# Moving a group norm off VectorE in a convolution kernel by codes

## The chip, the cores and the metric

The kernel runs on one core of a Trainium2 chip. The metric is device time in microseconds (us), the median of three runs; lower is better. Five engines work side by side, each with its own queue: TensorE (PE) for matrix products, VectorE (DVE), ScalarE (ACT), GpSimd (POOL) and SyncE (SP, which here only issues transfers). ScalarE and GpSimd issue transfers as well.

## The reference, cut to what matters

Sixteen images of 256 channels and 28x28 pixels. Each is normalised by groups of 8 channels, then passes two 3x3 convolutions by codes (every channel's 3x3 patch is softly assigned to 16 centroids), then a gate from channel means, and is added to the input.

```python
def amm_conv3x3(x, centroids, w_sub):
    p = patches(x, 3, 3)                                   # b, pixel, channel, 9
    d = sum(p*p) - 2*einsum('bncs,cks->bnck', p, centroids) + sum(centroids*centroids)
    attn = softmax(-d)                                     # over 16 centroids
    lut = einsum('cks,cso->cko', centroids, w_sub)
    return einsum('bnck,cko->bno', attn, lut)

def _gn(v, G=32, eps=1e-5):
    g = v.reshape(B, G, C // G, H, W)
    m, s = mean(g, (2, 3, 4)), var(g, (2, 3, 4))
    return (g - m) / sqrt(s + eps)

h   = _gn(x)
out = relu(bn1(amm_conv3x3(h, centroids1, wsub1)))
out = bn2(amm_conv3x3(out, centroids2, wsub2))
out = se_layer(out)                                        # channel gate
result = x + relu(out + h)
```

## The kernel before

The work is laid out in slots. A stage is one layer of one image: 2 pieces of 392 or so pixels times 11 groups of channels, 22 slots. Stages follow as layer 0 of image b+1, layer 1 of image b, and so on, 32 stages in all. In a slot TensorE computes the codes (`logits`), the numerators of the group before (`b_num`), and three or four "looks" (`c_look`, the product with the weights); ScalarE takes exponentials; VectorE transposes; GpSimd scales. Layer 1 needs the maximum of the codes first for three of its groups (`MAXED`): those are computed six slots ahead (`a_logits`, `a_turn`, `a_max`), which loads TensorE and above all VectorE in some slots.

```python
ring = [p_ring.tile([P, 2, 512], F32, name=f"pair{i}") for i in range(3)]   # PSUM, three pairs of banks
turn = [0]
def pair():
    turn[0] += 1
    return ring[turn[0] % 3]
def bank():
    return pair()[:, 0]
...
def logits(u, gi, rows):                        # two pairs of the ring
    ps = [pair(), pair()]
    ...
def a_turn(u, gi):                              # two transposes on VectorE
    for ps in u.pop(("lg", gi)):
        z = tpool.tile([P, 832], F32, tag="z", name="z")
        nc.vector.transpose(..., ps[:, :, : 32 * nb])
def b_exp(u, gi):
    for ps in u.pop(("lg", gi)):
        nc.scalar.activation(e[:, :, :n], ps[:, :, :n], AF.Exp, scale=2.0)
def b_num(u, gi):                               # one pair of the ring
    ps = pair()
    ...
def b_turn(u, gi):                              # on VectorE: transpose, reciprocal, two reductions
    ...
```

Group norm in four steps, one slot each, on VectorE with two small products on TensorE:

```python
def gn_stats(b):
    st = small.tile([P, NB, 2, 6], F32, name="gn_st")
    mv = small.tile([P, NB, 2], F32, name="gn_mv")
    for k in range(NB):                         # two blocks of 128 channels
        for i in range(2):
            nc.vector.bn_stats(st[:, k, i, :], xs[b][:, k, i * (HW // 2) : (i + 1) * (HW // 2)])
        nc.vector.bn_aggr(mv[:, k, :], st[:, k])
def gn_mean(b):
    ps = bank()[:, : 2 * NB]
    nc.tensor.matmul(ps, lhsT=gmat, rhs=mv, ...)
    nc.vector.tensor_copy(gm, ps)
    nc.vector.tensor_sub(dv, mv[:, :, 0], gm[:, :, 0])
    nc.vector.tensor_mul(dv, dv, dv)
def gn_var(b):
    ps = bank()[:, :NB]
    nc.tensor.matmul(ps, lhsT=gmat, rhs=dv, start=True, stop=True)
    nc.vector.tensor_add(var, gm[:, :, 1], ps)
    rsqrt(rstd, var, GN_EPS, NB)                # two operations on GpSimd
def gn_apply(b):
    for k in range(NB):
        nc.vector.tensor_scalar(ims[0][:, k, ...], xt[:, k], gm[:, k, 0:1], rstd[:, k : k + 1], op0=ALU.subtract, op1=ALU.mult)
```

The normed image is copied with a shift of one column to each side (`shift`, ScalarE) and written to memory as patterns (`to_pat`, transfers issued by ScalarE), from which `patches` (issued by GpSimd) loads the operands of the codes.

```python
class Plan:
    def prep(self, l, pat, t, near):
        for i, dx in enumerate((0, 2)):
            for k in range(NB):
                self.at(t + i, 4 + 2 * k, shift, l, dx, k)
        for i in range(len(STEPS)):             # 12 steps
            self.at(t + 1 + (i // 2 if near else i), 8, to_pat, l, i, pat)
    def norm(self, b, t):
        for k, f in enumerate((gn_stats, gn_mean, gn_var, gn_apply)):
            self.at(t + k, 9, f, b)
...
clear_pat(0)                                    # at the start: transfers issued by ScalarE
...
for f in (gn_stats, gn_mean, gn_var, gn_apply): # the first image, in the setup
    f(0)
...
        if l == 0 and b >= 1:
            t0 = t - NS + (1 if b == 1 else -6)
            plan.at(t0 - 1, 9, load_x, b, x[b])
            plan.norm(b, t0 + 1)
            plan.prep(0, pat_of(0, b), t0 + 5, False)
...
    plan.at(18, 9, setup_codes, 1)              # needs GpSimd and TensorE
```

`at(slot, pos, ...)` puts a step into a slot; steps of a slot go out in the order of `pos`, and each engine keeps that order.

Of the kernel before, what the change touches and what calls it, by code (L numbers as in the profile page):

```python
# [8 lines left out]
F32 = mybir.dt.float32  # L9
AF = mybir.ActivationFunctionType  # L10
ALU = mybir.AluOpType
# [4 lines left out]
P = 128  # L16
H = W = 28
HW = H * W
# [61 lines left out]
def kernel(  # L80
# [32 lines left out]
    nc = tc.nc  # L113
    B, C, _ = x.shape
    NB = C // P
# [5 lines left out]
    small = ctx.enter_context(tc.tile_pool(name="small", bufs=3))  # L121
# [8 lines left out]
    ring = [p_ring.tile([P, 2, 512], F32, name=f"pair{i}") for i in range(3)]  # L130
# [5 lines that stand above are left out]

    def bank():
        return pair()[:, 0]

    def view(t, off, dims):  # L140

        return bass.AP(t.tensor, t.offset + off, [list(d) for d in dims])

    d_pat = [dram.tile([NRT * 32, HW], F32, name=f"pat{i}") for i in range(3)]
# [4 lines left out]
    xs = {}  # L149

    def load_x(b, xb):
        t = xpool.tile([P, NB, HW], F32, tag="xt", name="xt")
        nc.gpsimd.dma_start(t, xb.rearrange("(b p) n -> p b n", p=P))
        xs[b] = t
# [52 lines left out]
    ims = [const.tile([P, NB, NPAD], F32, name=f"im{l}") for l in range(2)]  # L207
# [28 lines left out]
    def rsqrt(dst, src, eps, n):  # L236

        t = small.tile([P, n], F32, name="rs_t")
        nc.gpsimd.tensor_scalar(t, src, eps, None, op0=ALU.add)
        nc.gpsimd.tensor_tensor(dst, t, mhalf[:, :n], ALU.pow)  # L240
# [19 lines left out]
    def sort_channels():  # L260
# [12 lines left out]
        nc.vector.tensor_mul(key, key, t)  # L273

        ps = bank()
        for b in range(NB):
            dg = scratch(P)
# [136 lines left out]
    gst = {}  # L414
    nrm = {}

    def gn_stats(b):
        st = small.tile([P, NB, 2, 6], F32, name="gn_st")
        mv = small.tile([P, NB, 2], F32, name="gn_mv")
        for k in range(NB):  # L420
            for i in range(2):
                nc.vector.bn_stats(st[:, k, i, :], xs[b][:, k, i * (HW // 2) : (i + 1) * (HW // 2)])  # L422
            nc.vector.bn_aggr(mv[:, k, :], st[:, k])
        gst[b] = mv

    def gn_mean(b):
        mv = gst[b]
        ps = bank()[:, : 2 * NB]
        nc.tensor.matmul(ps, lhsT=gmat, rhs=mv.rearrange("p b t -> p (b t)"), start=True, stop=True)
        gm = small.tile([P, NB, 2], F32, name="gn_gm", bufs=6)  # L430
        nc.vector.tensor_copy(gm.rearrange("p b t -> p (b t)"), ps)
        dv = small.tile([P, NB], F32, name="gn_dv")
        nc.vector.tensor_sub(dv, mv[:, :, 0], gm[:, :, 0])
        nc.vector.tensor_mul(dv, dv, dv)
        gst[b] = gm, dv

    def gn_var(b):
        gm, dv = gst.pop(b)
        ps = bank()[:, :NB]
        nc.tensor.matmul(ps, lhsT=gmat, rhs=dv, start=True, stop=True)  # L440
        var = small.tile([P, NB], F32, name="gn_var")
        nc.vector.tensor_add(var, gm[:, :, 1], ps)
        rstd = small.tile([P, NB], F32, name="gn_rstd", bufs=6)
        rsqrt(rstd, var, GN_EPS, NB)
        nrm[b] = gm, rstd

    def gn_apply(b):
        gm, rstd = nrm[b]
        xt = xs.pop(b)
        for k in range(NB):  # L450
            nc.vector.tensor_scalar(
                ims[0][:, k, W : W + HW], xt[:, k], gm[:, k, 0:1], rstd[:, k : k + 1], op0=ALU.subtract, op1=ALU.mult
            )

    def shift(l, dx, k):

# [24 lines left out]
    se = {}  # L481

    def se_hidden(b):
        _, ysum = ys[b]
        ps = bank()[:, :1]
        n = 0
        for k in range(NB):
            for i in range(2):
                nc.tensor.matmul(
                    ps[0:RED], lhsT=w1_sb[:, k, :], rhs=ysum[:, k, i : i + 1],  # L490
                    start=(n == 0), stop=(n == 2 * NB - 1),
                )
                n += 1
        hid = small.tile([RED, 1], F32, name="se_hid")
        nc.scalar.activation(hid, ps[0:RED], AF.Relu, bias=b1_sb, scale=1.0 / HW)
        se[b] = hid

    def se_gate(b):
        hid = se.pop(b)
        ps = bank()[:, :NB]  # L500
        for k in range(NB):
            nc.tensor.matmul(
                ps[:, k : k + 1], lhsT=w2_sb[:, k * P : (k + 1) * P], rhs=hid, start=True, stop=True
            )
        gt = small.tile([P, NB], F32, name="se_gt")
        for k in range(NB):
            nc.scalar.activation(
                gt[:, k : k + 1], ps[:, k : k + 1], AF.Exp, bias=nb2_sb[:, k : k + 1], scale=-1.0
            )
        se[b] = gt  # L510

    def se_scale(b):
        gt = se[b]
        nc.vector.tensor_scalar_add(gt, gt, 1.0)
        nc.vector.reciprocal(gt, gt)
        gm, rstd = nrm[b]
        nb = small.tile([P, NB], F32, name="se_nb")
        nc.vector.tensor_mul(nb, gm[:, :, 0], rstd)
        nc.vector.tensor_scalar_mul(nb, nb, -1.0)
        se[b] = gt, nb  # L520

    def half(k, i):
        return slice(None), k, slice(i * (HW // 2), (i + 1) * (HW // 2))

    def gate(b, k, i):

        gt, nb = se[b]
        y = ys[b][0][half(k, i)]
        nc.scalar.activation(y, y, AF.Identity, bias=nb[:, k : k + 1], scale=gt[:, k : k + 1])  # L529

    def finish(b, k, i):

        y, xt = ys[b][0][half(k, i)], xs[b][half(k, i)]
        _, rstd = nrm[b]
        nc.vector.scalar_tensor_tensor(y, xt, rstd[:, k : k + 1], y, op0=ALU.mult, op1=ALU.add)  # L535
        nc.vector.scalar_tensor_tensor(y, y, 0.0, xt, op0=ALU.max, op1=ALU.add)  # L536

# [210 lines left out]
    NS = len(PXT) * NG  # L748
# [3 lines left out]
    class Plan:  # L752
# [59 lines left out]
        def prep(self, l, pat, t, near):  # L812
            for i, dx in enumerate((0, 2)):
                for k in range(NB):
                    self.at(t + i, 4 + 2 * k, shift, l, dx, k)
            for i in range(len(STEPS)):
                self.at(t + 1 + (i // 2 if near else i), 8, to_pat, l, i, pat)

        def norm(self, b, t):
            for k, f in enumerate((gn_stats, gn_mean, gn_var, gn_apply)):  # L820
                self.at(t + k, 9, f, b)

        def close(self, b, ob, te):
            self.at(te + 1, 9, se_hidden, b)
# [14 lines left out]
    def pat_of(l, b):  # L839
        if l == 0:  # L840
            return d_pat[2 if b == 1 else 0]
        return d_pat[0 if b == B - 1 else 1]

    for f in (gn_stats, gn_mean, gn_var, gn_apply):
        f(0)
    for i, (dx, pieces) in enumerate(STEPS):
        if dx != 1 and pieces == (0,):
            for k in range(NB):
# [21 lines left out]
    plan = Plan(4, 6)  # L870
    for t in exts:
        nc.vector.memset(t, 1.0)
    for si, (l, b) in enumerate(stages):
        t = si * NS
        plan.stage(l, b, pat_of(l, b), t, *((PAIRS, ()) if l == 0 else (MIXED, MAXED)), exts[si % 2])
        if l == 0 and b >= 1:
            t0 = t - NS + (1 if b == 1 else -6)
            plan.at(t0 - 1, 9, load_x, b, x[b])
            plan.norm(b, t0 + 1)
            plan.prep(0, pat_of(0, b), t0 + 5, False)  # L880
        if l == 1:
            near = b in (0, B - 1)
            plan.prep(1, pat_of(1, b), t - NS + (LC + 1 if near else 0), near)
            plan.at(t + NS + LC, 9, load_x, b, x[b])
            plan.close(b, out[b], t + NS + LC)
# [9 lines left out]
    ps = bank()  # L895
# [6 lines left out]
    with tc.If(flag > 0):  # L902
        with tc.For_i(0, B) as bi:
            load_x("g", x[bass.ds(bi, 1)].rearrange("o c n -> (o c) n"))
            plan = Plan(1, 4)
            plan.norm("g", 0)
            plan.prep(0, d_pat[0], 4, False)
            plan.stage(0, "g", d_pat[0], 30, PAIRS, ORDER, None)
            plan.prep(1, d_pat[1], 30 + NS + LC, False)
            s1 = 30 + NS + LC + 26  # L910
            plan.stage(1, "g", d_pat[1], s1, PAIRS, ORDER, None)
            plan.at(s1 + NS + LC, 9, load_x, "g", x[bass.ds(bi, 1)].rearrange("o c n -> (o c) n"))
            plan.close("g", out[bass.ds(bi, 1)].rearrange("o c n -> (o c) n"), s1 + NS + LC)
            plan.emit()
# [76 lines left out]
```

## Time and profile before

| | us |
|---|---|
| median of three runs | 3277.77 (3275.5 to 3278.19) |
| span of the profiled execution | 3267.5 |
| TensorE busy | 3106.2 |
| VectorE busy | 2527.0 |
| ScalarE busy | 1475.2 |
| GpSimd busy | 1313.0 |
| first codes of the first stage | at 106.80 |

The profile is one execution, read in several views. The engine table gives busy times; the slices show them along the span in tenths; the groups by line give count and mean duration of one kind of instruction; the timeline lists instructions in order (start, duration, engine, line, operation, output <- inputs, shape, count, and in brackets how long the engine had been idle and what ended that); the windows give busy time and granted TensorE clock in a stretch. Matrix products run pipelined, so a busy TensorE need not be at its full speed, and its lost time is best seen as the distance between the starts of its blocks.

### The profile page before, as it was taken

The numbers are of one execution on the slowest core, as the hardware profiler recorded it, in microseconds if no ns is written. First come the engines' busy times: TensorE is split into PE (matmuls) and PEld (weight loads), VectorE is DVE, ScalarE is ACT, GpSimd is POOL, SyncE is SP. The second block draws the span as 40 slices with busy tenths as digits, with TensorE's granted clock in tenths as the row PEclk, the third lists the DMA queues.
The fourth block names the chain that finished last, engine by engine and source line by source line (L and its number), as shares of the span: only waits on it lengthen the run. The fifth ranks groups of instructions, "written<-read, shape, count | busy, mean of one in ns | idle before, by whom it ended". The sixth has DMA issues, their size and how long they took to land.

```text
span 3267.5 us, 72362 instructions
## 1 busy us (share of the span) xinstructions
PE 3106.2 (95%) x29086; PEld 1214.2 (37%) x29086; DVE 2527.0 (77%) x4261; ACT 1475.2 (45%) x2443; POOL 1313.0 (40%) x1347
## 2 busy tenths in 40 slices
PE   4489999999999999999999999999999999999997
PEld 3133333333333333333333333333333333333333
DVE  2266878788787878878787887879788787878786
ACT  1144454444545444454444445444444545445343
POOL 1133444443434434343444434444443444434342
PEclk8699999999999999999999999999999999999999
DMA  7566555565655556565555656655565665556532
GB/s 239 122 183 198 179 183 183 156 204 172 219 184 172 188 156 195 181 213 178 172 182 155 218 177 202 192 164 187 155 226 177 195 194 163 181 166 218 175 104 69
DMA packets 232374, 586.03 MB, mean 179 GB/s; under 512 B 76238, under 2 KB 89182, under 8 KB 232030
## 3 DMA queue, kind: packets, MB, share of 16 engines
q0 software_dynamic: 76544, 321.16, 31.5%
q10 hardware_dynamic: 82666, 238.70, 22.2%
q1 hardware_dynamic: 72820, 21.45, 3.1%
q8 instruction: 232, 3.80, 0.5%
q14 instruction: 112, 0.92, 0.1%
HBM read 328.23 MB, written 257.82 MB: 179 GB/s over the span
## 4 chain that ended last, share of the span: by engine, by line
PE 73%; DVE 17%; DMA 5%; POOL 3%; issue 2%; ACT 1%; ACTq 0%; SPq 0%; POOLq 0%; DVEq 0%
PE acc L719 39%; PE pair L568 18%; PE pair L642 14%; DVE nt L654 4%; DVE q L708 3%; DVE rc L658 3%; POOL nt L681 3%; DVE y L535 2%; DMA xt<-in_x 1%; DMA pat<-side 1%; DVE gn_st L422 1%; DVE z L587 1%; DVE y L536 1%; DMA dm<-mt 1%; PE pair L336 1%
## 5 line engine op out<-in xcount | busy, mean ns | idle before, releaser
L719 PE MATMUL acc<-q,ws 128*128 128x384 f32 (+1 forms) x4608 | 1742.1, 513 | 0.5 <-ACT y L742 0.5
L632 ACT ACTIVATE e<-pair 128x768 f32<-128x768 f32 (+1 forms) x1408 | 1087.4, 822 | 1450.0 <-PE pair L568 1373.6
L681 POOL TENSOR_TENSOR nt<-nt,rc 128x648 f32<-128x648 f32 (+1 forms) x576 | 772.9, 1342 | 1466.4 <-DVE rc L658 1130.4
L719 PEld LDWEIGHTS acc<-q,ws 128*128 128x128 f32 x4608 | 814.2, 190 | 915.8 <-issue 470.2
L708 DVE STREAM_TRANSPOSE q<-nt 128x768 f32<-128x768 f32 (+1 forms) x576 | 578.5, 1004 | 413.9 <-POOL nt L681 367.6
L654 DVE STREAM_TRANSPOSE nt<-pair 128x768 f32<-128x768 f32 (+1 forms) x704 | 692.4, 983 | 143.4 <-PE pair L642 140.2
L642 PE MATMUL pair<-e,cw 64*32 64x384 f32 (+1 forms) x11264 | 641.8, 507 | 52.1 <-ACT e L632 43.4
L568 PE MATMUL pair<-pt,wd 31*64 31x384 f32 (+1 forms) x9216 | 564.3, 519 | 23.9 <-DVE z L587 23.9
L658 DVE RECIPROCAL rc<-nt 128x72 f32<-128x72 f32 (+1 forms) x704 | 438.5, 623 | 24.3
L687 POOL TENSOR_TENSOR qx<-nt,rc 128x324 f32<-128x324 f32 (+3 forms) x256 | 178.9, 737 | 392.0 <-DVE rc L658 392.0
L568 PEld LDWEIGHTS pair<-pt,wd 31*64 31x64 f32 x9216 | 144.7, 131 | 420.5 <-issue 343.3
L642 PEld LDWEIGHTS pair<-e,cw 64*32 64x32 f32 x11264 | 131.1, 105 | 422.3 <-ACT e L632 200.7
L697 ACT COPY nt<-qx 128x120 f32<-128x120 f32 (+1 forms) x576 | 184.4, 320 | 187.8 <-DVE rc L658 186.3
L553 POOL DMA_DIRECT2D pt<-pat x288 | 227.4, 790 | 43.6 <-DMA pat<-side 43.2
L568 PE MATMUL pair<-pm,wd 31*64 31x384 f32 (+1 forms) x3584 | 237.9, 513 | 4.4 <-DVE z L587 3.7
L587 DVE STREAM_TRANSPOSE z<-pair 128x768 f32<-128x768 f32 (+1 forms) x192 | 182.4, 987 | 67.3 <-PE pair L568 67.3
L593 DVE TENSOR_REDUCE mx<-z 128x48 f32<-128x768 f32 (+1 forms) x192 | 186.1, 969 | 0.0
L661 DVE TENSOR_REDUCE ext<-rc 128x1 f32<-128x72 f32 (+1 forms) x608 | 140.6, 231 | 20.8
L662 DVE TENSOR_REDUCE ext<-rc 128x1 f32<-128x72 f32 (+1 forms) x608 | 134.1, 221 | 0.0
L568 PEld LDWEIGHTS pair<-pm,wd 31*64 31x64 f32 x3584 | 60.7, 129 | 165.1 <-issue 66.6
L553 POOL DMA_DIRECT2D pm<-pat x128 | 95.3, 745 | 6.3 <-DMA pat<-side 6.3
L535 DVE SCALAR_TENSOR_TENSOR y<-xt,gn_rstd,y 128x392 f32<-128x392 f32 x64 | 76.9, 1202 | 0.8 <-ACT y L529 0.8
(105 smaller groups left out, 724.0 us busy)
## 6 DMA issues: line engine op xcount, KB each, us to landing
pt<-pat POOLq DMA_DIRECT2D x144, 800.0 KB, 7.4
pt<-pat POOLq DMA_DIRECT2D x144, 768.0 KB, 5.3
pat<-side ACTq DMA_DIRECT2D x128, 771.8 KB
pat<-im ACTq DMA_DIRECT2D x64, 771.8 KB
pat<-side ACTq DMA_DIRECT2D x64, 404.2 KB
pm<-pat POOLq DMA_DIRECT2D x64, 400.0 KB, 5.7
xt<-in_x POOLq DMA_DIRECT2D x32, 784.0 KB, 8.1
pm<-pat POOLq DMA_DIRECT2D x64, 384.0 KB, 4.3
```

The lines of the kernel that those rows point to most:

```text
L553: nc.gpsimd.dma_start(pt[:, : 2 * len(gs), :n], view(u["pat"], 2 * gs[0] * P * HW + px, [[HW, P], [P * HW, 2 * len(gs)], [1, n]]),)
L568: nc.tensor.matmul(ps[i // 2][64 * h : 64 * h + 64, i % 2, :n], lhsT=wd[l][32 * i : 32 * i + rows, 2 * g + h, :], rhs=u["pt"][32 * i : 32 ...
L587: nc.vector.transpose(z[:, : 64 * nb].rearrange("p (i m) -> p i m", i=2), ps[:, :, : 32 * nb])
L593: nc.vector.tensor_reduce(u["mx"][:, a : a + 2].rearrange("p i (c b) -> p i b c", c=2)[:, :, :nb], u["z", gi].pop(0)[:, : 64 * nb].rearran ...
L632: nc.scalar.activation(e[:, :, :n], ps[:, :, :n], AF.Exp, scale=2.0)
L642: nc.tensor.matmul(ps[32 * i : 32 * i + 32, h, :n], lhsT=cw[l][64 * h : 64 * h + 64, g, i, :], rhs=es[i // 2][64 * h : 64 * h + 64, i % 2, ...
L654: nc.vector.transpose(t[:, : 2 * nb].rearrange("p (h b) r -> p h (b r)", h=2), u.pop(("nm", gi))[:, :, : 32 * nb])
L658: nc.vector.reciprocal(rc[:, : 2 * nb], t[:, : 2 * nb, SUM : SUM + 3])
L681: nc.gpsimd.tensor_tensor(v, v, rc[:, : 2 * nb].unsqueeze(3).to_broadcast([P, 2 * nb, 3, 9]), ALU.mult)
L697: nc.scalar.copy(u["nt", gi][0][:, : 2 * nb].rearrange("p (h b) r -> p h b r", h=2)[:, :, :, SUM:], bass.AP(w.tensor, w.offset, [list(w.ap ...
L708: nc.vector.transpose(q[:, : 64 * nb], t[:, : 2 * nb].rearrange("p b r -> p (b r)"))
L719: nc.tensor.matmul(accs[key][:, :n], lhsT=ws[l][:, 2 * g + h, o * P : (o + 1) * P], rhs=u["q", gi][:, 32 * nb * h : 32 * nb * h + n], star ...
```

## The change

Group norm is taken apart and moved. The statistics are taken block by block in two slots instead of in one, with the second in a slot that has no maxima before or in it. The pass over the image becomes an activation on ScalarE (`rstd * x + nb`), for which `nb = -mean * rstd` is computed once and shared with the gate. The small steps go from VectorE to ScalarE (copies out of PSUM) and GpSimd (arithmetic). The small products of group norm and gate no longer take a new pair of the ring: they use the second bank of the pair taken last (`spare`), which the exponentials have just read, so the ring keeps its turn. The shifts move to the end of a slot, behind its exponentials, and the patterns of image 1 are written in six slots instead of twelve.

```diff
+    def spare():
+        return ring[turn[0] % 3][:, 1]
...
-    def gn_stats(b):
-        ...
-        for k in range(NB):
-            for i in range(2):
-                nc.vector.bn_stats(st[:, k, i, :], ...)
-            nc.vector.bn_aggr(mv[:, k, :], st[:, k])
+    def gn_stats(b, k):
+        ...
+        for i in range(2):
+            nc.vector.bn_stats(st[:, i, :], xs[b][:, k, i * (HW // 2) : (i + 1) * (HW // 2)])
+        nc.vector.bn_aggr(gst[b][:, k, :], st)
     def gn_mean(b):
-        ps = bank()[:, : 2 * NB]
+        ps = spare()[:, : 2 * NB]
         nc.tensor.matmul(ps, lhsT=gmat, ...)
-        nc.vector.tensor_copy(gm, ps)
+        nc.scalar.copy(gm, ps)
-        nc.vector.tensor_sub(dv, mv[:, :, 0], gm[:, :, 0])
-        nc.vector.tensor_mul(dv, dv, dv)
+        nc.gpsimd.tensor_sub(dv, mv[:, :, 0], gm[:, :, 0])
+        nc.gpsimd.tensor_mul(dv, dv, dv)
     def gn_var(b):
-        ps = bank()[:, :NB]
+        ps = spare()[:, :NB]
-        nc.vector.tensor_add(var, gm[:, :, 1], ps)
+        nc.scalar.copy(var, ps)
+        nc.gpsimd.tensor_add(var, var, gm[:, :, 1])
         rsqrt(rstd, var, GN_EPS, NB)
+        nc.gpsimd.tensor_mul(nb, gm[:, :, 0], rstd)
+        nc.gpsimd.tensor_scalar(nb, nb, -1.0, None, op0=ALU.mult)
-    def gn_apply(b):
-        for k in range(NB):
-            nc.vector.tensor_scalar(ims[0][...], xt[:, k], gm[:, k, 0:1], rstd[:, k : k + 1], op0=ALU.subtract, op1=ALU.mult)
+    def gn_apply(b, k):
+        nc.scalar.activation(ims[0][...], xs[b][:, k], AF.Identity, bias=nb[:, k : k + 1], scale=rstd[:, k : k + 1])
...
     def se_hidden(b):          # and se_gate
-        ps = bank()[...]
+        ps = spare()[...]
     def se_scale(b):
         ...
-        nc.vector.tensor_mul(nb, gm[:, :, 0], rstd)
-        nc.vector.tensor_scalar_mul(nb, nb, -1.0)
...
     def prep(self, l, pat, t, near):
-                    self.at(t + i, 4 + 2 * k, shift, l, dx, k)
+                    self.at(t + 1 + i, 8, shift, l, dx, k)
     def norm(self, b, t):
-        for k, f in enumerate((gn_stats, gn_mean, gn_var, gn_apply)):
-            self.at(t + k, 9, f, b)
+        self.at(t, 9, gn_stats, b, 0)
+        self.at(t + 2, 9, gn_stats, b, 1)
+        self.at(t + 3, 9, gn_mean, b)
+        self.at(t + 4, 9, gn_var, b)
+        self.at(t + 5, 8, gn_apply, b, 0)
+        self.at(t + 6, 8, gn_apply, b, 1)
...
-            t0 = t - NS + (1 if b == 1 else -6)
-            plan.at(t0 - 1, 9, load_x, b, x[b])
-            plan.norm(b, t0 + 1)
-            plan.prep(0, pat_of(0, b), t0 + 5, False)
+            t0 = t - NS + (1 if b == 1 else -5)
+            plan.at(t0 - 2, 9, load_x, b, x[b])
+            plan.norm(b, t0)
+            plan.prep(0, pat_of(0, b), t0 + 6, b == 1)
```

## The prediction

> **What bounds the kernel now.** I read the page's engine table and slices first, then the groups by line and shape, the timeline around a group norm beside one stretch without it, the windows for the granted clock, and last the timeline of the setup.
>
> ```profile
> PE 3106.2 (95%) x29086; PEld 1214.2 (37%) x29086; DVE 2527.0 (77%) x4261; ACT 1475.2 (45%) x2443; POOL 1313.0 (40%) x1347
> ...
> PE   4489999999999999999999999999999999999997
> ```
>
> TensorE (PE) is busy 95% of 3267.5 us. The idle part is mostly in the first three slices, the setup. After it a slice is at 9, so a change on other engines can only win back what PE still loses. In a calm stretch a block of 16 products has one fixed length, so the losses can be counted: this is PE in the first layer of the last image, beside which no further image is left to normalise, from the numerators of slot 18 to those five slots on.
>
> ```profile
> 3011.74 0.91 PE L642 MATMUL pair<-e,cw 64*32 64x400 f32 x16
> 3012.58 1.21 PE L568 MATMUL pair<-pt,wd 31*64 31x400 f32 x16
> 3013.71 1.61 PE L719 MATMUL acc<-q,ws 128*128 128x400 f32 x4
> ...
> 3032.82 0.88 PE L642 MATMUL pair<-e,cw 64*32 64x384 f32 x16
> ```
>
> These five slots take 3032.82 - 3011.74 = 21.08 us. The same five slots, taken likewise from the timeline in the 14 stages that hold a group norm (images 2 to 15), take 23.85 to 28.58, mean 25.92. So group norm costs 4.84 us an image and 14 x 4.84 = 67.7 us in all: that is the ceiling of the change in the steady part. Here is where it goes, in an image without a dropped clock:
>
> ```profile
> 2053.06 1.03 DVE L422 BATCH_NORM_STATS2 gn_st<-xt 128x6 f32<-128x392 f32 x2
> ...
> 2053.93 0.91 PE L642 MATMUL pair<-e,cw 64*32 64x400 f32 x16
> ...
> 2055.39 1.79 DVE L587 STREAM_TRANSPOSE z<-pair 128x768 f32<-128x768 f32 x2
> ...
> 2056.37 1.76 PE L568 MATMUL pair<-pt,wd 31*64 31x400 f32 x16 [1.53 <-DVE z L587]
> ```
>
> The statistics stand at the end of slot 17 (slots counted in the stage), just ahead of slot 18, whose maxima pass needs two transposes (z) on VectorE (DVE). Those start 2.33 us late (2053.06 to 2055.39), and the codes' products (L568) wait for them, as their two ring pairs are the ones being transposed. Numerators to codes is 2.44 us here against 0.84 in the calm stretch, codes to looks 1.70 against 1.13: 1.60 + 0.57 = 2.17 lost to 2.33 us of VectorE work. Nearly one for one, so VectorE has no slack in these slots.
>
> ```profile
> 511.00:521.00 10.00, 8.46 (x73) 0.83 0.27 85
> ...
> 895.00:906.00 11.00, 8.92 (x72) 0.71 0.27 79
> ...
> 2052.00:2062.00 10.00, 8.47 (x90) 1.00 0.27 85
> ...
> 3008.00:3018.00 10.00, 9.90 (x95) 1.00 0.26 85
> ```
>
> These are windows of PE over the statistics: length, PE busy, granted clock. The first two lost clock as well as time; 9 of the 14 do (0.71 to 0.85), four stay at 1.00, the first has 0.98.
>
> [...]
>
> **The change part by part.** *VectorE, per image.* Removed: two passes (L451) of 1.182 = 2.36, the copy of the means 0.16, the two operations for dv 0.23 + 0.16, the variance add 0.15, and the two nb operations at the gate 0.21 + 0.17; 3.4 us in sum, 55 us over 16 images. Kept: statistics, 4 x 0.545 + 2 x 0.209 = 2.6 us of records, 2.33 end to end.
>
> *The statistics in two slots.* Block 0 stays at the end of slot 17, block 1 goes to the end of slot 19. The z of slot 18 starts 1.17 us sooner, and of the 2.17 lost there 1.0 remains. The other 1.17 us sits in front of slot 20, which has no maxima but follows a slot whose second maximum (0.95) and mt transpose (0.31) come late; slot 21 has its own two transposes. Adding VectorE's durations in order from slot 18's transposes (q 1.0, nt 1.0, reciprocal 0.64, ext 0.45, maximum 0.95 each) puts the nt of slot 20 about 0.8 us after PE wants that pair. I book 0.7 us for slot 21 over the calm stretch. Before, slots 19 to 21 lost more in such an image: 25.08 - 21.08 = 4.0, less 2.17, leaves 1.8.
>
> *The pass and the small ones.* On ScalarE 784 elements cost 0.712 + 392 x 0.875 ns = 1.06 us, an estimate; the slope is that of L742, (695 - 681) / 16 ns an element. They fall in slots 22 and 23, one each. ScalarE has about 1.1 us free between a slot's fill and the next exponentials (887.14 to 888.16 in one, filled there by other work), and exponentials end some 0.5 us before the looks. So it nearly fits; I book 0.3 us for it and for the two shifts that now stand together in one slot (2 x 0.82). The two small products stay on PE, 0.42 together. GpSimd gets five operations of about 0.22, 1.1 us an image, at 40% busy: nothing. The bank of the last exponentials no longer turns the ring, so codes don't wait for a small VectorE copy; that is inside the 1.8 above.
>
> *Late input.* In four images the statistics start late as x is still arriving. The load keeps its slot (15), so this stays: 0.3 us a mean image, with the clock drops that remain.
>
> Sum over the calm stretch: 1.0 + 0.7 + 0.3 + 0.4 + 0.3 = 2.7 instead of 4.84. Gain 2.1 x 14 = 30 us.
>
> *The first stage.* Image 1 gets its patterns in half as many slots (8 to 13 instead of 7 to 18). Before, GpSimd waited for the last of them ahead of the code setup, and PE for GpSimd:
>
> ```profile
> 213.31 1.38 POOL L681 TENSOR_TENSOR nt<-nt,rc 128x702 f32<-128x702 f32 x1 [2.18 <-DVE rc L658]
> 219.77 0.79 POOL L553 DMA_DIRECT2D pt<-pat  x1 [5.08 <-DMA pat<-side]
> 220.58 2.23 POOL L399 TENSOR_TENSOR sq<-wd 128x352 f32<-128x352 f32 x3
> ```
>
> That gives back 5.1 us and about 1 us of half clock. But where the kernel already writes patterns at the doubled rate (283 to 299 us), exponentials waited 4.63 and 5.49 us behind ScalarE's own issues, and PE's blocks lost some 5 us. Net -1 us.
>
> *The setup.* The first group norm's copies now stand in ScalarE's queue behind the clearing of the patterns:
>
> ```profile
> 3.79 20.24 ACTq L167 DMA_DIRECT2D pat<-in_consts  x6
> 24.14 11.33 ACTq L474 DMA_DIRECT2D pat<-im  x5
> ```
>
> VectorE copied the means at 16.98 and had the normed image at 21.72, before ScalarE's queue was free at 24.03. Now the chain starts at 24.05: copy 0.2, dv 0.45, product 0.6, copy 0.3, add 0.2, rsqrt 1.0, nb 0.45, two passes 2.1 = 5.3, so the first pattern leaves at about 29.5, not 24.14. ScalarE's queue then holds the weight copies (PE waited 11.3 us for L328), so most of 5.4 reaches the end; loads that use the free transfer engines meanwhile give some back. I book +4 us.
>
> Total: 3277.8 - 30 - 1 + 4 = 3251.
>
> **Rivals.** *ScalarE becomes the bound.* Passes (2.1 us), copies (0.4) and paired shifts delay exponentials, and PE waits for those instead. For: exponentials have only 0.5 us of slack in a slot of six look products. Against: ScalarE is 45% busy, and in the contested slots VectorE is late anyway, so the waits overlap. Fully paid, 14 x 2.5 = 35 us eat the gain: about 3285. *The loss disappears.* If 1.17 us of VectorE at a time is absorbed, and with shorter stalls no clock is lost, 14 images cost only the 0.42 of products: 14 x 4.4 = 62 gained, time 3219. [...] Against: one-for-one loss in slot 18. *The statistics only move their wait.* If slot 21 pays the full 1.17 and more, each image gains what the pass cost, about 1.3: 18 us, time 3263.
>
> **Range and chances.** Centre 3251. The steady gain is 15 to 50 us by the rivals, setup and first stage together 0 to +9. That gives 3228 to 3270. Over 2% faster needs below 3213.5, past even the second rival: 0.04. Over 2% slower needs above 3343, for which I see no mechanism: 0.02. Within 2%: 0.94.
>
> **What would show it.** The five slots should take about 23.8 us instead of 25.92, with 1.0 us still lost at slot 18's codes on z, and fewer than five images with a dropped clock. VectorE busy should fall by some 55 us, ScalarE rise by about 40. In the setup the first pattern issue (24.14) should come near 29.5, and the first codes (106.80) about 4 us later. PE's 7.91 us wait for sq should fall to about 3. I am wrong if the five slots stay over 25 us with exponentials as what PE waits for, if they fall under 22, or if the setup does not move.

## The result and the profile after

| | before | after |
|---|---|---|
| median, us | 3277.31 | 3248.85 (3242.53 to 3254.78) |
| ratio, 95% interval | | 0.9914 (0.989 to 0.9937) |
| span of the profiled execution | 3267.5 | 3240.9 |
| first codes | 106.80 | 116.43 |
| stage 0, its numerators to those of stage 1 | 134.37 | 141.06 |
| stages 2 to 29, likewise | 2686.2 | 2644.7 |
| stages 1 and 30, and stage 31 to the end of the span | 337.9 | 336.5 |

The changed kernel is 28.5 us faster, 0.9%; 3251 was predicted. The rows below the span split the profile: 9.6 and 6.7 us are lost ahead of stage 1, 41.5 us are won in stages 2 to 29. (The 2.2 us from the first codes to the first numerators are in no row, and are the same in both.) The last row's 1.4 us were not followed up. Here is the page, engine table and TensorE's slices:

```profile
PE 3079.0 (95%) x29086; PEld 1208.6 (37%) x29086; DVE 2479.0 (76%) x4133; ACT 1506.0 (46%) x2507; POOL 1330.1 (41%) x1427
...
PE   3489999999999999999999999999999999999997
```

VectorE lost 48.0 us of busy time and ScalarE gained 30.8. TensorE has the same 29086 products in 27 us less, and its first slice has gone from 4 to 3: the setup is what became longer.

The timeline around the statistics, in an image whose input was in time:

```profile
2230.71 1.03 DVE L426 BATCH_NORM_STATS2 gn_st<-xt 128x6 f32<-128x392 f32 x2
...
2231.58 0.90 PE L645 MATMUL pair<-e,cw 64*32 64x400 f32 x16
...
2231.90 1.79 DVE L590 STREAM_TRANSPOSE z<-pair 128x768 f32<-128x768 f32 x2
...
2232.88 1.77 PE L571 MATMUL pair<-pt,wd 31*64 31x400 f32 x16 [0.40 <-DVE z L590]
...
2234.58 1.61 PE L722 MATMUL acc<-q,ws 128*128 128x400 f32 x4
```

VectorE is 1.19 us behind slot 18 (2230.71 to 2231.90) and no longer 2.33. Numerators to codes is 1.30 us, 0.46 over the calm stretch; codes to looks 1.70, 0.57 over. Together 1.03 are lost. In the view of the waits, TensorE's waits for z fell from 27.6 us (20 waits) to the first of these lines (us in total, times, longest):

```profile
PE pair L571 <- DVE z L590: 10.5, 14, 1.8
...
PE pair L571 <- DVE nt L657: 5.4, 14, 0.5
```

The kernel before has the second of these waits once (0.5 us). Here it belongs to the second block, in slot 20 of 13 of the 14 images (all but the one that loses its clock):

```profile
2242.03 0.99 DVE L426 BATCH_NORM_STATS2 gn_st<-xt 128x6 f32<-128x392 f32 x2
...
2244.11 1.01 DVE L657 STREAM_TRANSPOSE nt<-pair 128x832 f32<-128x832 f32 x1
...
2244.51 0.28 PE L432 MATMUL pair<-gn_mv,gmat 128*128 128x4 f32 x2
2245.17 0.91 PE L571 MATMUL pair<-pm,wd 31*64 31x384 f32 x16 [0.38 <-DVE nt L657]
```

The block stands ahead of the transpose nt, and TensorE's next codes wait for nt. From its numerators to those of slot 21, slot 20 takes 6.17 us, 5.60 in the calm stretch. The five slots take 23.30 us on average over the 14 images, before 25.92; the calm stretch is unchanged (21.09). The windows over the statistics (length, PE busy, granted clock, DMA share, GB/s):

```profile
527.00:537.00 10.00, 9.60 (x93) 1.00 0.35 95
...
904.00:914.00 10.00, 9.08 (x92) 1.00 0.28 88
...
2039.00:2050.00 11.00, 9.60 (x88) 0.84 0.30 83
```

The third is the only one of 14 with a dropped clock; before there were nine. Now ScalarE's timeline in the setup ("ACTq" is its transfer queue):

```profile
3.80 19.11 ACTq L171 DMA_DIRECT2D pat<-in_consts  x6
22.95 0.16 ACT L434 COPY gn_gm<-pair 128x4 f32<-128x4 f32 x1 [20.64 <-DMA pat<-in_consts]
...
26.55 1.97 ACT L456 ACTIVATE im<-xt,gn_nb,gn_rstd 128x784 f32<-128x784 f32 x2 [2.04 <-POOL gn_nb L451]
27.62 6.63 ACTq L481 DMA_DIRECT2D pat<-im  x5
```

The copy of the means came at 22.95, behind the clearing of the patterns (before, VectorE's came at 16.98), and the first pattern left at 27.62, not 24.14. And in the first stage:

```profile
198.96 8.05 ACTq L481 DMA_DIRECT2D pat<-side  x3
207.11 1.57 ACT L635 ACTIVATE e<-pair 128x800 f32<-128x800 f32 x2 [10.32 <-DMA pat<-side]
```

Three pattern issues held ScalarE, which computed nothing for 10.32 us ahead of these exponentials, and TensorE lost 10.5 us in slots 12 to 15. Against that stands the wait that the doubled rate was to remove:

```profile
237.65 2.95 POOL L403 TENSOR_TENSOR sq<-wd 128x352 f32<-128x352 f32 x4
238.49 4.33 PE L405 MATMUL pair<-sq,nhalf_sb 128*128 128x352 f32 x8 [2.53 <-POOL sq L403]
```

It fell from 7.91 to 2.53 us, half of what the late exponentials cost.

### The profile page after: what moved, and what is told of

It is laid out like the page before. It is cut to its first block, busy times and chain, and to the rows that moved or that the text cites. A ratio compares the mean times of both kernels' runs of the same rounds, so it can differ in the third digit from the quotient of the medians.

```text
span 3240.9 us, 72313 instructions
## 1 busy us (share of the span) xinstructions
PE 3079.0 (95%) x29086; PEld 1208.6 (37%) x29086; DVE 2479.0 (76%) x4133; ACT 1506.0 (46%) x2507; POOL 1330.1 (41%) x1427
## 4 chain that ended last, share of the span: by engine, by line
PE 70%; DVE 17%; DMA 6%; POOL 3%; issue 2%; ACT 1%; SPq 0%; ACTq 0%; POOLq 0%; DVEq 0%
PE acc L722 38%; PE pair L571 17%; PE pair L645 13%; DVE nt L657 4%; DVE q L711 4%; POOL nt L684 3%; DVE rc L661 3%; DVE y L538 2%; DMA xt<-in_x 1%; DVE z L590 1%; DMA pat<-in_consts 1%; DVE gn_st L426 1%; DVE y L539 1%; DMA ws<-dws 1%; DMA dm<-mt 1%
## 5 line engine op out<-in xcount | busy, mean ns | idle before, releaser
L571 PE MATMUL pair<-pm,wd 31*64 31x384 f32 (+1 forms) x3584 | 224.9, 513 | 6.9 <-DVE nt L657 5.4
```

Source lines behind the costliest of these rows:

```text
L571: nc.tensor.matmul(ps[i // 2][64 * h : 64 * h + 64, i % 2, :n], lhsT=wd[l][32 * i : 32 * i + rows, 2 * g + h, :], rhs=u["pt"][32 * i : 32 ...
```

## The experiments

Times are medians, beside the kernel before on the same chip, with the 95% interval of the ratio. The stage lengths of each profile are used to place a difference, as a median moves by several us between runs (those of the changed kernel lie from 3242.53 to 3254.78). They have a spread too: the changed kernel, E1, E2 and E12 share one steady part and took 2643.9 to 2651.3 us in stages 2 to 29, so a smaller difference there is read from single slots, each from its numerators to those of the next. All edits are to the changed kernel. There is no E8.

### E1: the first image's group norm on VectorE again

```diff
-    gn_mean(0); gn_var(0)                     # and gn_apply(0, k): ScalarE and GpSimd
+    nc.vector.tensor_copy(gm0, ps0)           # the operations of the kernel before,
+    nc.vector.tensor_sub(dv0, ...)            # products in spare()
+    ...
+    nc.vector.tensor_scalar(ims[0][...], xs[0][:, k], gm0[...], rstd0[...], op0=ALU.subtract, op1=ALU.mult)
```

> The changed kernel with one part undone: the group norm of the first image, in the setup, is done by VectorE as before; all later images as changed. My theory: the setup of the changed kernel is 9.6 us longer (first codes at 115.9 instead of 106.3 us) as the copies stand behind ScalarE's transfers, GpSimd's chain holds up the code setup, and the loads of the weight parts, which share its buffers, then meet the pattern writes. First codes should come back to 106 to 107 us, and the time fall by 8 to 10 us, to about 3239 (0.9885 of before). Rival: the delay comes from the two passes on ScalarE and the order of the shifts alone, and the weight parts are late for another reason; then under 5 us come back.

3245.53 us (0.9914, 0.9889 to 0.9938). The first codes came at 110.13 us, 6.3 us earlier than in the changed kernel, but not at the 106 to 107 expected; stages 2 to 29 took 2643.9. Its setup:

```profile
24.14 11.79 ACTq L481 DMA_DIRECT2D pat<-im  x5
...
57.44 0.93 ACT L332 COPY ws<-pair 128x256 f32<-128x256 f32 x3 [12.99 <-DMA pat<-side]
```

The first pattern leaves at 24.14 as before, and the weight copies come at 57.44 instead of 61.91. The median alone, 3 us lower, would show nothing. But four kernels of this study have the first image on VectorE (first codes 107.05 to 112.62, mean 110.0) and eight have it on ScalarE and GpSimd (115.17 to 118.66, mean 116.9), and the two sets don't overlap: the place of this group norm costs 6.9 us. The other 3 us to the 106.80 of the one profile of before are less than the spread of the first set (5.6).

### E2: image 1's patterns in twelve slots

```diff
-            t0 = t - NS + (1 if b == 1 else -5)
+            t0 = t - NS + (0 if b == 1 else -5)
...
-            plan.prep(0, pat_of(0, b), t0 + 6, b == 1)
+            plan.prep(0, pat_of(0, b), t0 + 6, False)
```

> The changed kernel with the patterns of image 1 written in twelve slots (7 to 18) again instead of six; group norm of that image one slot earlier to make room. My theory: writing at double rate fills ScalarE's transfer queue, and exponentials wait behind it (10.3 us at one place), which costs stage 0 some 11 us, while the wait of GpSimd that it was to remove cost 5 to 6. Expected: stage 0 about 134 to 136 us instead of 141, time 5 to 7 us lower, about 3243. Rival: the wait of GpSimd for the last pattern (5.1 us, and TensorE's 7.9 behind it) comes back in full and nothing is gained: 3249, within 2 us.

3242.0 us (0.9895, 0.9873 to 0.9918); stage 0 took 135.79 us instead of 141.06, as the theory of the blocked ScalarE had it (5.3 us less). Over all runs the eight kernels with six slots have 137.84 to 145.33 (mean 141.0), the four with twelve (three of them with other moves as well) 132.14 to 135.79 (mean 134.3), and before had 134.37. So the doubled rate costs the first stage 6.7 us net of the wait that it shortens.

### E3: the pass on VectorE again, in the same slots

```diff
-        nc.scalar.activation(ims[0][...], xs[b][:, k], AF.Identity, bias=nb[...], scale=rstd[...])
+        nc.vector.tensor_scalar(ims[0][...], xs[b][:, k], rstd[...], nb[...], op0=ALU.mult, op1=ALU.add)   # b >= 1
```

> The changed kernel with the pass over the image on VectorE again for images 1 to 15 (same slots, 22 and 23, one block each; one operation with rstd and nb). My theory: VectorE has no slack between slots 18 and 36, where layer 1's maxima stand every third slot, so 2.4 us of VectorE work per image cost 1 to 2 us of TensorE: 14 to 28 us more, 3263 to 3277. Rival: the gain came from splitting the statistics and from the bank, and the pass is free in these slots: under 4 us more.

3263.32 us (0.9964, 0.9949 to 0.998); stages 2 to 29 took 2663.6, 18.9 more. The timeline shows where:

```profile
2089.19 0.96 DVE L461 TENSOR_SCALAR im<-xt,gn_rstd,gn_nb 128x784 f32<-128x784 f32 x1
...
2090.96 1.84 DVE L595 STREAM_TRANSPOSE z<-pair 128x768 f32<-128x768 f32 x2
...
2091.99 1.74 PE L576 MATMUL pair<-pm,wd 31*64 31x384 f32 x16 [0.65 <-DVE z L595]
```

This is slot 24, the first of the next stage with maxima. VectorE reaches its transposes late, behind the pass and a small step that E9 brings up, and the codes wait. The slot takes 4.72 us and not 3.60: 1.12 x 14 = 15.7 of the 18.9. The rest is in the five slots (23.52), in images whose input was late.

### E4: both blocks of statistics in one slot

```diff
-        self.at(t + 2, 9, gn_stats, b, 1)
+        self.at(t, 9, gn_stats, b, 1)
```

> The changed kernel with both blocks' statistics at the end of slot 17 again, all else as changed. My theory: the second block's 1.17 us stands in front of slot 18's two transposes and costs 1.0 to 1.2 us there, and the longer stall brings back the dropped clock in more than half of the images, 1.3 to 2 us each: five slots go from 23.3 to 25 us, 16 to 28 us in all, time 3265 to 3277. Rival: the split only moves the loss to slot 21, and the gain came from taking the pass away: under 6 us more.

3278.82 us (1.0012, 1.0002 to 1.0022): the whole gain is gone. Stages 2 to 29 took 2675.5, 30.8 more, nearly all of it in the five slots (25.46). They are still 10.7 us shorter than before; the setup and the first stage take that back. From TensorE's timeline, in an image whose input was in time:

```profile
2447.22 0.90 PE L645 MATMUL pair<-e,cw 64*32 64x400 f32 x16
2449.67 1.97 PE L571 MATMUL pair<-pt,wd 31*64 31x400 f32 x16 [1.54 <-DVE z L590]
2451.57 3.04 PE L722 MATMUL acc<-q,ws 128*128 128x400 f32 x4
```

TensorE waits 1.54 us for z instead of 0.40, and behind that wait its clock drops: four looks take 3.04 us instead of 1.61. In 13 of the 14 images (all but image 2) the clock drops, behind waits of 1.53 to 2.76 us, for example in these two windows:

```profile
2066.00:2077.00 11.00, 9.60 (x68) 0.84 0.41 139
2256.00:2266.00 10.00, 8.20 (x71) 0.83 0.34 96
```

With no block in slot 19, slot 20 takes 5.72 us and not 6.17, and its codes do not wait for nt: there the split costs 0.45 us.

### E5: the small products take a pair of the ring again

```diff
     def spare():
-        return ring[turn[0] % 3][:, 1]
+        return bank()
```

> The changed kernel with the small products in a new pair of the ring again, so the ring turns by one at each of the four small products of an image; all else as changed. My theory: the two pairs that the next codes need are then the one just transposed and the one whose small product ScalarE must first read; ScalarE's copy comes after its fill and is early enough, so the five slots stay within 0.5 us of 23.3 and the time within 6 us of 3249. Rival: the bank was a main part of the gain (slot 19 lost 0.4 to 0.9 us before and nothing now): five slots over 24 us, time over 3258.

3248.69 us (0.9915, 0.9891 to 0.9938). Stages 2 to 29 took 2653.1, 8.4 more, while the median is that of the changed kernel: a few us, no more. The wait for nt in slot 20 now stands ahead of the product of the means, which had been done while TensorE waited:

```profile
2250.01 0.39 PE L432 MATMUL pair<-gn_mv,gmat 128*128 128x4 f32 x2 [0.50 <-DVE nt L657]
```

So slot 20 takes 6.48 us, 0.31 more. Slot 21 takes 0.14 less, slot 24 0.21 more. Over 13 images that is 5 us; the rest of the 8.4 lies in slots 18 and 19.

### E6: the shifts ahead of the exponentials again

```diff
-                    self.at(t + 1 + i, 8, shift, l, dx, k)
+                    self.at(t + 1 + i, 4 + 2 * k, shift, l, dx, k)
```

> The changed kernel with the four shifts of an image at their old places in the slot (one ahead of the exponentials, one with them), in the slots that the change gives them. My theory: in the middle of the run ScalarE has room for them either way, so the stages stay at 94.3 to 94.4 us and the time within 5 us of 3249. Rival: shifts ahead of exponentials hold up TensorE now that ScalarE has the pass and the copies too: 0.5 us an image and layer or more, 15 us.

3238.94 us (0.9888, 0.9858 to 0.9919); stages 2 to 29 took 2643.2, 1.5 less. The place of the shifts neither costs nor brings anything that shows.

### E7: the input one slot earlier

```diff
-            plan.at(t0 - 2, 9, load_x, b, x[b])
+            plan.at(t0 - (2 if b == 1 else 3), 9, load_x, b, x[b])
```

> The changed kernel with the input of images 2 to 15 loaded one slot earlier (14 instead of 15). My theory: what slot 18 loses beyond 1.31 us in some images (1.8 to 3.9) is the input arriving after VectorE is ready for it, and the dropped clock behind that. With the earlier load every image should have 23.0 us in its five slots, mean 23.0 instead of 23.3, and no dropped clock there: 4 to 6 us less, about 3244. Rival: the input is not what is late (the load waits for the buffer or for GpSimd all the same), or the clock drops from a stall of 1.3 us by itself: some images stay over 23.3.

3243.43 us (0.9905, 0.9882 to 0.9928). VectorE's waits for the input, in the changed kernel and here:

```profile
DVE gn_st L426 <- DMA xt<-in_x: 10.9, 5, 7.5
```

```profile
DVE gn_st L426 <- DMA xt<-in_x: 8.1, 1, 8.1
```

The one that is left is the setup's. The five slots now take 23.0 us in nearly every image (mean 23.03), no image loses clock, and stages 2 to 29 take 4.7 us less: late input, with the clock dropped behind it, had cost the 13 images there 0.38 us each. Stage 1 takes 106.5 us and not 103.1, which was not followed up.

### E9: the statistics two slots later

With E1 and E2 in it, so that only the steady part is asked:

```diff
-        self.at(t + 2, 9, gn_stats, b, 1)     # and the four steps after it
+        self.at(t + 3, 9, gn_stats, b, 1)     # each one later
...
-            t0 = t - NS + (1 if b == 1 else -5)
-            plan.at(t0 - 2, 9, load_x, b, x[b])
+            t0 = t - NS + (-1 if b == 1 else -3)      # slots 19 and 22, not 17 and 19
+            plan.at(t0 - (2 if b == 1 else 4), 9, load_x, b, x[b])     # the input still in slot 15
```

> A kernel meant to beat both: the changed kernel with the first image's group norm on VectorE in the setup, image 1's patterns in twelve slots, and the two blocks' statistics at the ends of slots 19 and 22, each a slot after a second maximum and before a slot without maxima, with the rest of group norm three slots later. My theory: what follows such a slot takes 1.17 us of VectorE work at no cost (slot 21 loses 0.33 in the changed kernel, against 0.29 with no group norm), so slot 18 loses 0.3 instead of 1.3 us or more and the input is never late: five slots about 21.6 us, at most 0.4 us more at slot 24. Gain over the changed kernel 14 x 1.4 = 20 us, plus 6 in the setup and 5 in stage 0: about 3218. Rival: VectorE has no slack anywhere between slots 18 and 36, and each block costs 1 us wherever it stands; then only the 11 us of setup and stage 0 come: about 3238.

3232.92 us (0.9877, 0.9853 to 0.9901): less of a gain than expected. Slot 18 takes no more than in the calm stretch (3.51 us) and the five slots take 21.67, but stages 2 to 29 are at 2645.7, no better than the changed kernel. The blocks are not free: slot 20 takes 6.17 us (5.60 in the calm stretch) and slot 23, outside the five, 6.81 (6.22), both with a wait for nt (28 of these 29):

```profile
PE pair L571 <- DVE nt L657: 13.2, 29, 0.8
```

Most of the loss has moved to slot 24, which takes 4.69 us instead of 3.60:

```profile
2049.98 0.99 DVE L426 BATCH_NORM_STATS2 gn_st<-xt 128x6 f32<-128x392 f32 x2
...
2053.95 0.17 DVE L673 TENSOR_REDUCE ext_t<-ext 128x1 f32<-128x22 f32 x1
...
2054.59 0.58 DVE L674 TENSOR_TENSOR worst<-worst,ext_t 128x1 f32<-128x1 f32 x1
...
2055.09 1.83 DVE L590 STREAM_TRANSPOSE z<-pair 128x768 f32<-128x768 f32 x2
...
2056.12 1.74 PE L571 MATMUL pair<-pm,wd 31*64 31x384 f32 x16 [0.49 <-DVE z L590]
```

Between the second block and slot 24's transposes stands a small step that nobody had looked at: at the end of each stage the "watch" reduces the stage's extremes (L673 and L674, twice each), 1.14 us of VectorE in slot 23 (2053.95 to 2055.09).

### E10: E9, and the watch four slots later

```diff
-                at(s0 + NS + 1, 9, watch, ext)
+                at(s0 + NS + 5, 9, watch, ext)
```

> The run with the statistics at slots 19 and 22, with one more move: the watch over the ends of the sums (two reductions and two small operations, 1.2 us of VectorE) four slots later, from slot 23 to slot 27. My theory: the second block lost what the first gained because slot 23 held the watch, so that 2.4 us stood ahead of slot 24's transposes; with the watch gone from there slot 24 should lose 0.3 to 0.5 us instead of 1.39, and two stages together 187.4 to 187.9 us instead of 188.96: 14 to 20 us less, about 3216. Rival: VectorE is full from slot 18 to 36 and the watch costs as much at slot 27, ahead of slot 29: no change in two stages, 3233.

3217.93 us (3217.29 to 3221.89; 0.9831, 0.9814 to 0.9848), the fastest of this study and below both kernels. Without the watch between them:

```profile
2045.94 0.99 DVE L426 BATCH_NORM_STATS2 gn_st<-xt 128x6 f32<-128x392 f32 x2
...
2049.95 1.85 DVE L590 STREAM_TRANSPOSE z<-pair 128x768 f32<-128x768 f32 x2
...
2051.52 1.21 PE L571 MATMUL pair<-pm,wd 31*64 31x384 f32 x16
```

The codes at 2051.52 wait for nothing, slot 24 takes 3.74 us (the second product is in it; the calm stretch has 3.49), and stages 2 to 29 take 2632.6, 13.1 less than in E9. One move of a step of 1.14 us did it. The waits for nt in slots 20 and 23 stay.

### E11: the statistics earlier instead, in slots 16 and 19

With E1 and E2 in it, the watch in its old place:

```diff
-        self.at(t + 2, 9, gn_stats, b, 1)     # and the four steps after it
+        self.at(t + 3, 9, gn_stats, b, 1)     # each one later
...
-            t0 = t - NS + (1 if b == 1 else -5)
+            t0 = t - NS + (-1 if b == 1 else -6)
```

> Another place for the statistics: slots 16 and 19 (the input loaded in slot 14, group norm's end one slot before that of the changed kernel, watch unmoved), with the first image on VectorE and image 1's patterns in twelve slots. My theory: slot 17 has no maxima and takes most of the first block's 1.17 us (VectorE needs about 3.1 us in such a slot, TensorE 3.9 to 4.5), so slot 18 loses 0.3 to 0.7 instead of 1.31: five slots 22.0 to 22.4 instead of 23.0, two stages 187.6 to 188.1. Rival: slot 17 has no room left and slot 18 loses 1.3 again: two stages 188.6.

3236.36 us (0.9891, 0.9875 to 0.9908): missed, for a reason in neither theory. The five slots did fall to 22.03, but slot 17 now loses 1.68 us. The waits of VectorE, and one image:

```profile
DVE gn_st L426 <- DMA xt<-in_x: 62.5, 15, 31.6
```

```profile
2023.48 1.04 DVE L426 BATCH_NORM_STATS2 gn_st<-xt 128x6 f32<-128x392 f32 x2 [1.42 <-DMA xt<-in_x]
```

The load had moved to slot 14 with the statistics two slots behind it, and there the input is late in all of images 3 to 15, which E7's three slots were enough to avoid.

### E12: the setup of the codes ahead of the first group norm

```diff
+    setup_codes(0)
     for k in range(NB):
         gn_stats(0, k)
...
-    setup_codes(0)
```

> The changed kernel with only the order of the setup changed: the code setup of layer 0 (GpSimd squares, TensorE products, VectorE adds) stands ahead of the first image's group norm, whose small steps stay on ScalarE and GpSimd. My theory: of the 9.6 us that the setup lost, the late pattern start explains 3.5 and the rest comes from the weight loads, which share buffers with the code setup and so started at 30 instead of 23 us and met the pattern writes. With the code setup first the loads should start before 23 us, the first pattern at about 27.6 as in the changed kernel, and the first codes come at 109 to 112 us instead of 116.4. Rival: the late patterns alone hold up ScalarE's weight copies: first codes stay at 115 to 118.

3244.44 us (0.9908, 0.9887 to 0.9929); first codes at 115.79: missed. In the changed kernel the loads of the weight parts, which share buffers with what GpSimd squares for the codes, began at 30.05 us, in E1 at 22.85. The question was whether that delay is what moves the end of the setup.

```profile
23.19 44.52 SPq L320 DMA_DIRECT2D part<-in_ws  x5
...
34.35 6.16 ACTq L481 DMA_DIRECT2D pat<-im  x5
...
61.40 0.92 ACT L332 COPY ws<-pair 128x256 f32<-128x256 f32 x3 [8.49 <-DMA pat<-side]
```

The loads did begin at 23.19, but the first pattern now left at 34.35, and ScalarE's weight copies came at 61.40, as late as in the changed kernel. With the loads early and the patterns 6.7 us later still the end is the same. Both were moved at once, so how much of the 6.9 us is due to either stays open.

## Why the prediction was right, and where it was right by luck

3251 was predicted and 3248.85 measured, but two of the three terms of its sum were mis-sized, and in opposite directions: "Gain 2.1 x 14 = 30 us" brought 41.5, and "Net -1 us" with "I book +4 us", +3 together, came as +16.3. The errors of 11.5 and 13.3 us cancelled. The first lies within what the range had allowed it ("15 to 50"), the second outside ("0 to +9"). (By these two ranges the upper end would be 3272, not 3270.)

**Right: slot 18.** "Nearly one for one" holds. Of 2.17 us, 1.03 remain (1.0 predicted), and E4 puts them back by undoing the split alone.

**Right in kind: the second block.** "I book 0.7 us" came as 0.45, and where the working had seen it: the nt of slot 20 is late. (The text on the change calls slot 19 free of maxima; the second maximum stands in it, just ahead of the block, as the prediction says.) In the 13 images of stages 3 to 27 the five slots take 23.40 us, 2.31 over the calm stretch: 1.03 in slot 18, 0.42 more there for late input and clock (0.3 predicted), 0.53 in slot 20 and 0.33 in slot 21. The last two hold the second block and the small products, which take 0.12 (slot 20 in E4) and 0.33 (0.4 predicted). ScalarE's 0.3 did not come: slots 22 and 23, which hold the passes, take 3.88 and 6.22 us as in the calm stretch.

The pass was worth taking away. In the kernel before it stood ahead of slot 21's transposes:

```profile
2259.83 2.31 DVE L451 TENSOR_SCALAR im<-xt,gn_gm,gn_rstd 128x784 f32<-128x784 f32 x2
...
2262.06 1.83 DVE L587 STREAM_TRANSPOSE z<-pair 128x768 f32<-128x768 f32 x2
...
2263.08 1.76 PE L568 MATMUL pair<-pm,wd 31*64 31x400 f32 x16 [0.47 <-DVE z L587]
```

Slot 21 took 4.61 us there, 3.52 in the calm stretch, and takes 3.84 now, product included.

**Missed: slot 24.** The prediction counted the five slots of the statistics and nothing behind them. Slot 24 took 4.06 us before and takes 3.60 now: 0.46 x 14 = 6.4 us that the sum had not. They are not group norm's own loss, for in the calm stretch slot 24 takes 4.10. What stands ahead of its transposes is the watch: in E10, without it, the calm stretch has 3.49. In the changed kernel VectorE starts those transposes 0.63 us ahead of TensorE's numerators, before 0.17, so the watch is better hidden. The likely reason is that the second product now holds up TensorE, and not VectorE, in slot 21; no run tests that alone. The other 13 images' five slots (the 14th lies in stage 1) give 13 x 2.68 = 34.8, and with 6.4 that is the 41.5 measured, within 0.3.

**Right in kind: the clock.** "Fewer than five images with a dropped clock" came as one. It belongs to the gain of the split: in E4, with the stall back, 13 of 14 drop. But "with shorter stalls no clock is lost", on which one rival rested, does not hold: the last section has the clock lost after a wait of 1.40 us and kept after one of 1.79.

**Mis-sized: the first stage.** "PE's blocks lost some 5 us" became 10.5. That figure came from a place of the kernel before where exponentials waited 4.63 and 5.49 us behind issues; in the first stage three issues came in a row and kept ScalarE from computing for 10.32. The other half was right: the wait for sq fell by 5.4, and its slot took 6.1 less: those 5.4, and 0.7 as the products behind the wait took 4.33 us and not 5.06 (the granted clock was 0.64 from 220 to 230 us before, and 0.83 from 236 to 246 now). 6.1 had been booked, with the "half clock" as 1.0 of it. E2 shows the sum, 6.7 us against the change.

**Mis-sized: the setup.** The chain on ScalarE was even shorter than predicted (first pattern at 27.62, not 29.5), and yet the first codes came 9.6 us later, not 4. "Most of 5.4 reaches the end" is the step that failed: the first pattern left 3.5 us later than before, and 6.9 us reached the end. GpSimd's share of the chain also held its work for the codes (from 19.48 to 26.48), and with it the weight loads. E1 and the two sets of kernels show that these 6.9 us come from the place of this group norm; which path carries them, E12 could not tell.

**The rivals.** ScalarE did not become the bound: its pass came at 1.040 us (1.06 predicted, from 0.712 us, the median of the gate's 392 elements, L529 of the kernel before), and E6 shows slack for the shifts. The statistics moved only part of their wait: the split took 1.14 us from slot 18 and gave 0.45 to slot 20. E4 and E3 give 30.8 us for the split, with the clock, and 18.9 for the pass on VectorE in its new slots, where it stood ahead of the watch. With 8.4 for the bank (E5) and -1.5 for the shifts these are more than the 41.5 won, so they overlap and don't add up. The loss did not disappear in the changed kernel, but E10 shows that most of it can: 53.6 us won in stages 2 to 29 (that rival had 62 for the steady part). It was not absorbed, as the rival had it, but the blocks stand where each costs some 0.5 us, in slots 20 and 23.

**Busy times.** VectorE fell by 48.0 us (55 predicted) and ScalarE rose by 30.8 (40); why both are less was not followed up.

## What to carry to other kernels

When the bound engine waits for another, what a step costs depends on what stands behind it. Here a block of 1.17 us cost 1.14 us just ahead of slot 18's transposes, and some 0.5 at the end of slot 19 or 22. So cut such a step, put the parts where least is due, and then look at what else stands in the slots between, down to a step of 1 us; and count the slots behind it, not only its own. A step moved to an engine that also issues transfers can wait behind them: here ScalarE's copy of the means came at 22.95 us, behind the clearing of the patterns, and exponentials at 207.11, after 10.32 us without work behind three pattern issues. So look at its transfer queue in the setup and in the first stage, not at its busy share. And compare a prediction term by term: a total that fits may be two errors.

## What the runs showed of the hardware

A dropped clock adds some 1.4 us to a stall (four looks in 3.04 us, not 1.61), but the length of one wait doesn't decide it. Waits of 1.53 to 1.56 us at slot 18 kept the clock in four images of the kernel before (one of them at 2056.37) and lost it in five, and in E4 they lost it every time; looks then ran 0.67 us apart (1094.92 to 1095.59 in the kernel before), not 0.34. The changed kernel kept the clock after a wait of 1.79 and lost it, in the third window above, after 1.40:

```profile
1474.98 1.76 PE L571 MATMUL pair<-pt,wd 31*64 31x400 f32 x16 [1.79 <-DVE z L590]
1476.67 1.61 PE L722 MATMUL acc<-q,ws 128*128 128x400 f32 x4
...
2043.06 1.96 PE L571 MATMUL pair<-pt,wd 31*64 31x400 f32 x16 [1.40 <-DVE z L590]
2044.95 3.04 PE L722 MATMUL acc<-q,ws 128*128 128x400 f32 x4
```

What tells a wait that costs the clock from one that doesn't stays open.

ScalarE's activations with both scale and bias from tiles take 716 ns in the mean for 392 elements (L532 of the changed kernel) and 1040 for 784 (L456). An estimate from these two means is 0.827 ns an element and 392 ns fixed.
